# Tokens sorted into couples of passes that share a matrix, a first product by features, and a first tile that is turned before it is centred

## The chip, the cores and the metric

The kernel runs on one core of a Trainium2 chip. Its time is the device time of one execution in microseconds; the median of three runs before the change is 277.46 us (276.93 to 278.12). A core has five engines, each with its own queue that is worked in order: TensorE (PE; its weight loads are PEld), VectorE (DVE), ScalarE (ACT), GpSimd (POOL) and SyncE (SP), and 16 DMA engines that all queues share.

## The reference

There are 2,048 tokens of 512 features, and four matrices of 512x512, `ctx_2048[e]`. The first half is a gated product in which a token's id picks its matrix, used three times; the second half is a routed feed-forward layer. Cut to what is computed:

```python
x = x + tanh(g_xattn[0]) * xattn(layernorm(x), itok, ctx, ctx, ctx)
x = x + tanh(g_ffn[0]) * ffn(layernorm(x), w1, w3, w2, wr)

def xattn(h, token_ids, Wg, Wu, Wd):     # Wg = Wu = Wd = ctx, 4 experts
    e = minimum(clip(token_ids, 0, 24999) // 6250, 3)
    for each expert e:                   # tokens of other experts keep their own
        g = silu(h @ Wg[e].T); u = h @ Wu[e].T
        out[tokens of e] = (g * u) @ Wd[e].T

def ffn(x, w1, w3, w2, wr):
    p = softmax(x @ wr.T);  r, idx = top_k(p, 2);  gates = r / sum(r)
    h = silu(silu(x @ w1.T) @ w3.T) @ w2.T
    for k in range(2):
        out = out.at[idx[:, k]].add(gates[:, k:k+1] * h)   # idx is 0 to 7
```

Since g and u use one matrix, with z = h @ W.T the middle is silu(z) * z. The last loop adds into rows 0 to 7 of the output alone.

## The kernel before

**Sorting.** The core counts the tokens of each expert and gives each token a place, so that whole tiles of 128 places belong to one expert. There are 17 passes of 128 places: 13 with one expert (numbers below `NF` = 13) and 4 mixed ones, in which each quarter of 32 places has its own expert. The sums that give the places are a row of small VectorE steps (L205 to L253); `padded` is the place of each token. Then the compares `at_lane` (L258) and `what` (L267, L270) make one-hot tables, and 16 small matmuls into `tok` (L276) turn them round, so that `from_row` (L286) holds the token number of each lane of each pass. `which0` (L245) and `which` (L300) hold the matrix's first row for each place. `busy(n)` puts in n matmuls whose result nobody reads.

**A pass** p of the gated product has these steps, each a function:

- `gather(p)`: POOL fetches the pass's 128 token rows by an indirect DMA into x (pool `xp`, five buffers); `load(p)`: SP reads the matrix number and starts the load of one matrix of 1 MB, or four (pool `mp`, seven buffers).
- `centre(p)`: VectorE takes the moments of x and subtracts the mean: h. `scale` and `norms` work out the inverse root of the variance, rs, in a chain of nine small VectorE steps (`inverse_roots`, L355 to L373); in the loop two chains, for two tiles, are interleaved.
- `turn_in(p)`: TensorE turns h by four transposes (tp_a), ScalarE copies them to hT. The first tile has a form of its own, `first_in` (L415 to L428), in two halves.
- `up(p)`: z = h @ W.T by `expert_product` (L453): four matmuls with the turned tokens as the stationary operand and 512 columns of the matrix moving; the profile has two records for each. A mixed pass has sixteen, with 32 tokens each. Then ScalarE's Silu (L466), with rs as its scale, and VectorE's product with z and rs (L467): g.
- `turn_mid(p)`: TensorE turns g (tp_g), ScalarE copies it to gT (L473).
- `down(p)`: y = gT's product with the same matrix, VectorE adds it to x (L481), POOL stores the rows (L482).
- `norms(p_in, p_out)`: the moments of the new x, the two inverse roots (for this tile and for the one that comes in), and the normed tile h_f (L505). `turn_out(p)` turns it (tp_f), and ScalarE copies it to hT2, from which the feed-forward layer works.

**The order of the work** is written out by hand and is the order of each engine's queue. After the first two passes, a loop over i does, for the i-th pass of the list `order`: `up(i)`, `turn_in(i+1)`, `centre(i+2)`, `gather(i+3)`, `load(i+3)`, `down(i-1)`, `turn_out(i-2)`, `norms(i+2, i-1)`, `turn_mid(i)`. `step()` mixes in parts of the feed-forward layer as soon as half of the tokens are there (from i = 10): first layer by seven products of sums (`first_layer`, whose w1 sums are made in rounds 5 to 8), then `second_layer`, whose last part is the end of the kernel. w1 and wr are loaded in round 2, w3 and w2 in round 7. `tg` (tanh of the two gates) is a ScalarE step that waits for two tiny loads.

Of the kernel before, what the change touches and what calls it, by code (L numbers as in the profile page):

```python
# [19 lines left out]
P = 128  # L20
# [5 lines left out]
def tile_gated_moe_ffn(  # L26
# [39 lines left out]

    nc = tc.nc
# [7 lines left out]
    NF = NJ - (E - 1)  # L75
    G = P // Q
# [8 lines left out]
    mp = ctx.enter_context(tc.tile_pool(name="mp", bufs=7))  # L85
    xp = ctx.enter_context(tc.tile_pool(name="xp", bufs=5))
# [11 lines left out]
        "lane", "atlane12", "atlane4", "passes", "what", "place", "over", "rank_in", "incl",  # L98
        "keep", "cum", "hot", "before", "later", "stepped", "behind", "ones", "place0", "number",
        "idt", "pad", "psum", "padded", "lanes", "inpass",  # L100
# [26 lines left out]
    ones_f = ct_([P, 2 * E], F32, "ones_f")  # L127
    nc.vector.memset(ones_f, 1.0)
    extra = ct_([P, 2, E], F32, "extra")
    nc.vector.memset(extra[:, 0, :], 0.0)  # L130
    nc.vector.memset(extra[:, 1, :], float(Q - 1))
    whole = ct_([P, 2, E], I32, "whole")
    nc.vector.memset(whole[:, 0, :], -P)
    nc.vector.memset(whole[:, 1, :], -Q)
    cut = ct_([P, 2 * E + 1], F32, "cut")
# [5 lines left out]
    steps = ct_([P, 2 * E - 1], F32, "steps")  # L141
    nc.vector.memset(steps, float(D))
    nc.vector.memset(steps[:, E - 1 : E], float(-(E - 1) * D))
# [7 lines left out]
    H = 12  # L151
# [46 lines left out]
    def busy(n):  # L198
# [12 lines left out]
    num = ct_([P, 2, E], I32, "num")  # L211
    nc.vector.tensor_tensor(
        num, incl[:, :, NJ - 1].unsqueeze(1).to_broadcast([P, 2, E]), extra, ALU.add
    )

    size = ct_([P, 3, E], I32, "size")
    nc.vector.tensor_tensor(size[:, 0:3:2, :], num, whole, ALU.bitwise_and)
    nc.vector.tensor_sub(size[:, 1, :], size[:, 2, :], size[:, 0, :])

    def wide(a):  # L220
# [6 lines left out]
        cut[:, 1 : 2 * E + 1], ones_f, size[:, 0:2, :].rearrange("p h e -> p (h e)"),  # L227
        0.0, ALU.mult, ALU.add,
# [3 lines left out]
    over = ct_([P, E, NJ], F32, "over")  # L232
    nc.vector.tensor_tensor(over, rank_in, wide(size[:, 0, :]), ALU.is_ge)
    jump = ct_([P, E], F32, "jump")
    nc.vector.tensor_sub(jump, cut[:, E : 2 * E], cut[:, 1 : E + 1])
    place = ct_([P, E, NJ], F32, "place")
    nc.vector.tensor_tensor(place, rank_in, wide(cut[:, 0:E]), ALU.add)
    nc.vector.tensor_tensor(over, over, wide(jump), ALU.mult)

    start = ct_([P, 2 * E - 1], F32, "start")  # L240
    nc.vector.scalar_tensor_tensor(start, cut[:, 1 : 2 * E], 0.0, steps, ALU.is_le, ALU.mult)
    nc.vector.tensor_add(place, place, over)
    which0 = ct_([P, 1], I32, "which0")
    with nc.allow_low_precision("whole numbers below 4096"):
        nc.vector.tensor_reduce(which0, start, AX.X, ALU.add)  # L245
    nc.vector.tensor_mul(place, place, hot)
# [7 lines left out]
    atlane = [ct_([P, P, n], F16, f"atlane{n}") for n in (H, NJ - H)]  # L254

    def at_lane(h):
        j, n = (0, H) if h == 0 else (H, NJ - H)
        return nc.vector.tensor_tensor(  # L258
            atlane[h],
            lane[:, :, 0:n],  # L260
            lanes[:, j : j + n].unsqueeze(1).to_broadcast([P, P, n]),
            ALU.is_equal,
        )

    at_lane(0)
# [7 lines left out]
    at_lane(1)  # L273
    tok = ps_x.tile([P, NP], F32, tag="x", name="tok")
    for j in range(NJ):
        nc.tensor.matmul(  # L276
            tok, atlane[j // H][:, :, j % H], what[:, :, j], start=(j == 0), stop=(j == NJ - 1)
        )

    which = ct_([P, NU], I32, "which")  # L280
    later = ct_([P, 2 * E, NU], F32, "later")
    stepped = ct_([P, 2 * E - 1, NU], F32, "stepped")

    busy(21)
# [4 lines left out]
        place0.unsqueeze(1).to_broadcast([P, 2 * E, NU]),  # L289
        cut[:, 1 : 2 * E + 1].unsqueeze(2).to_broadcast([P, 2 * E, NU]),  # L290
# [4 lines left out]
        later[:, 0 : 2 * E - 1],  # L295
        steps.unsqueeze(2).to_broadcast([P, 2 * E - 1, NU]),
# [8 lines left out]
    def row_tables():  # L305
# [6 lines left out]
        nc.vector.tensor_sub(pads, size[:, 2, :], num[:, 0, :])  # L312
# [3 lines left out]
            later[:, E : 2 * E, NF:NU],  # L316
# [21 lines left out]
    def moments(xt, name):  # L338
        st = small.tile([P, 6], F32, tag="st", name=f"st_{name}")
        nc.vector.bn_stats(st, xt)  # L340
        mv = small.tile([P, 2], F32, tag="mv", name=f"mv_{name}")
        nc.vector.bn_aggr(mv, st)
        return mv

    def inverse_roots(mvs_, names):


        n = range(len(names))

        def new(tag):  # L350
            return [small.tile([P, 1], F32, tag=tag, name=f"{tag}_{name}") for name in names]

        v, r, q, w, rs = new("v"), new("r"), new("q"), new("w"), new("rs")
        for i in n:
            nc.vector.tensor_scalar_add(v[i], mvs_[i][:, 1:2], EPS)  # L355
        for i in n:
            nc.vector.tensor_scalar(
                r[i].bitcast(I32), v[i].bitcast(I32), -0.5, float(0x5F3759DF), ALU.mult, ALU.add
            )
        for i in n:  # L360
            nc.vector.scalar_tensor_tensor(q[i], r[i], v[i], r[i], ALU.mult, ALU.mult)
        for i in n:
            nc.vector.tensor_scalar(w[i], q[i], 0.375, -1.25, ALU.mult, ALU.add)
        for i in n:
            nc.vector.tensor_scalar(w[i], w[i], q[i], 1.875, ALU.mult, ALU.add)
        for i in n:
            nc.vector.tensor_mul(r[i], r[i], w[i])
        for i in n:
            nc.vector.scalar_tensor_tensor(q[i], r[i], v[i], r[i], ALU.mult, ALU.mult)
        for i in n:  # L370
            nc.vector.tensor_scalar(q[i], q[i], -0.5, 1.5, ALU.mult, ALU.add)
        for i in n:
            nc.vector.tensor_mul(rs[i], r[i], q[i])  # L373
        return rs
# [8 lines left out]
    order = [0, 1, 2, 3, 4, 5, NF, 6, 7, 8, NF + 1, 9, 10, NF + 2, 11, 12, NF + 3]  # L383
    assert sorted(order) == list(range(NP))
    xs, x1s, mvs, rss, hs, hTs, gTs, gs, hs2, mats = {}, {}, {}, {}, {}, {}, {}, {}, {}, {}

    def gather(p):
        xt = xp.tile([P, D], F32, tag="x", name=f"x_{p}")
        nc.gpsimd.indirect_dma_start(  # L389
            out=xt,  # L390
            out_offset=None,
            in_=x,
            in_offset=bass.IndirectOffsetOnAxis(ap=from_row[:, p : p + 1], axis=0),
        )
        xs[p] = xt

    def centre(p):

        mvs[p] = moments(xs[p], f"a{p}")
        hs[p] = work.tile([P, D], F32, tag="h", bufs=4, name=f"h_a{p}")  # L400
        nc.vector.tensor_scalar(hs[p], xs[p], mvs[p][:, 0:1], None, ALU.subtract)  # L401

    def scale(*ps):
        for p, rs in zip(ps, inverse_roots([mvs.pop(p) for p in ps], [f"a{p}" for p in ps])):
            rss[p] = rs
# [6 lines left out]
    def first_in(p):  # L412

        st = small.tile([P, 6], F32, tag="st", name=f"st_a{p}")
        nc.vector.bn_stats(st, xs[p])  # L415
        mvs[p] = small.tile([P, 2], F32, tag="mv", name=f"mv_a{p}")
        nc.vector.bn_aggr(mvs[p], st)
        hTs[p] = work.tile([P, KC * P], F32, tag="hT", bufs=2, name=f"hT_{p}")
        n = D // 2
        for i in range(2):  # L420
            h = work.tile([P, n], F32, tag="h", bufs=4, name=f"h_a{p}_{i}")
            nc.vector.tensor_scalar(
                h, xs[p][:, i * n : (i + 1) * n], mvs[p][:, 0:1], None, ALU.subtract
            )
            tp = ps_tp.tile([P, n], F32, tag="tp", name=f"tp_a{p}_{i}")
            for k in range(n // P):
                nc.tensor.transpose(tp[:, k * P : (k + 1) * P], h[:, k * P : (k + 1) * P], ident)
            nc.scalar.copy(hTs[p][:, i * n : (i + 1) * n], tp)  # L428

    def load(p):  # L430

        n0, n = (p, 1) if p < NF else (NF + (p - NF) * G, G)
        mats[p] = []
        for i in range(n0, n0 + n):
# [9 lines left out]
            mats[p].append(m)  # L444
# [16 lines left out]
    def up(p, inside=None):  # L461
        z = ps_mm.tile([P, D], F32, tag="mm", name=f"z_{p}")
        expert_product(z, hTs.pop(p), p, inside)
        g = work.tile([P, D], F32, tag="g", bufs=2, name=f"g_{p}")
        rs = rss.pop(p)
        nc.scalar.activation(g, z, AF.Silu, scale=rs)  # L466
        nc.vector.scalar_tensor_tensor(g, z, rs, g, ALU.mult, ALU.mult)  # L467
        gs[p] = g

    def turn_mid(p):  # L470
        tp = transposed(gs.pop(p), f"g{p}")
# [20 lines left out]
    def norms(p_in, p_out):  # L492


        if p_out is None:
            return
        xt = x1s.pop(p_out)
        mv = [moments(xt, f"f{p_out}")]
        names = [f"f{p_out}"]
        if p_in is not None:  # L500
            mv.append(mvs.pop(p_in))
            names.append(f"a{p_in}")
        rs = inverse_roots(mv, names)
        h = work.tile([P, D], F32, tag="h", bufs=4, name=f"h_f{p_out}")
        nc.vector.tensor_scalar(h, xt, mv[0][:, 0:1], rs[0], ALU.subtract, ALU.mult)  # L505
        hs2[p_out] = h
        if p_in is not None:
            rss[p_in] = rs[-1]
# [212 lines left out]
    def second_layer(b, g):  # L721
# [61 lines left out]
        a = work.tile([P, D], F32, tag="g", bufs=2, name="a")  # L783
# [52 lines left out]
    row_tables()  # L836
    positions.close()
# [125 lines left out]
```

## Time and profile before

| | before |
|---|---|
| time, median of three runs | 277.46 us (276.93 to 278.12) |
| profiled execution | 277.53 us |
| its span, first to last instruction | 275.8 us |
| granted TensorE clock | 1.00 |
| first gather issued, landed | 9.35, 12.87 us |
| first product z begins | 15.44 us |
| first product y begins | 24.02 us |
| output tile ready | 272.65 us |
| DMA | 42.54 MB, of it 29 matrices of 1 MB |

Times within the profile count from the start of the span. "Busy" is the time in which an engine works on an instruction. The chain of work is followed back from the last instruction: at each step to what released it, or to the instruction before it on its engine. In names, out<-in are the program's tiles; `128*128 128x512` is a stationary operand of 128 rows and columns and a moving one of 512 columns. An x after a name counts records.

### The profile page before, as it was taken

What the parts mean: (1) busy time and instruction counts of PE and PEld (TensorE: products, weight loads), DVE (VectorE), ACT (ScalarE), POOL (GpSimd) and SP (SyncE); (2) the same over time, 40 slices, a digit from 0 to 9 for tenths busy, and PEclk for the clock granted to TensorE, in tenths of its full rate; (3) what the DMA queues carried; (4) which work ended last, traced back from release to release, by engine and by line L of the source; (5) the groups of instructions that cost most, each with busy time, mean ns of one, the idle gap of its engine ahead of it and who ended that gap; (6) DMA issues with size and microseconds to landing.
All of it is one profiled execution on the core that took longest, in us unless ns stands there. A gap on an engine that the chain in (4) does not pass through costs nothing.

```text
span 275.8 us, 3562 instructions
## 1 busy us (share of the span) xinstructions
PE 266.6 (97%) x1173; PEld 125.4 (45%) x1173; DVE 148.7 (54%) x593; ACT 69.3 (25%) x134; POOL 39.3 (14%) x63
## 2 busy tenths in 40 slices
PE   5889999999999999999999999999999999999994
PEld 2445455544355454444344444534245444344362
DVE  6677877777888769918263481516253620711000
ACT  2022232232232231223143232312113233311120
POOL 6520122221122211211110010101010000000000
PEclk9999999999999999999999999999999999999999
DMA  0697998545669996697304084001000000000000
GB/s 1 217 354 277 408 402 334 173 155 206 228 225 402 389 409 258 173 398 264 112 26 166 2 312 180 38 0 40 0 12 2 0 0 1 0 0 2 0 0 2
DMA packets 20722, 42.54 MB, mean 154 GB/s; under 512 B 2143, under 2 KB 2207, under 8 KB 20704
## 3 DMA queue, kind: packets, MB, share of 16 engines
q1 hardware_dynamic: 17952, 33.66, 34.0%
q0 software_dynamic: 2720, 8.65, 8.3%
q8 instruction: 9, 0.15, 0.2%
q14 instruction: 9, 0.07, 0.1%
q10 hardware_dynamic: 32, 0.01, 0.0%
HBM read 38.10 MB, written 4.47 MB: 154 GB/s over the span
## 4 chain that ended last, share of the span: by engine, by line
PE 94%; DVE 2%; DMA 2%; issue 1%; ACT 0%; DVEq 0%
PE z L453 22%; PE y L453 21%; PE v L730 20%; PE X L622 10%; PE Y L622 5%; PE tp_f L380 3%; PE tp_a L380 3%; PE tp_g L380 3%; PE Z L622 2%; PE acc L742 1%; PE lg L699 1%; DMA x<-in_x_dram,from_row 1%; DMA idt<-in_ids_dram 1%; PE accT L758 1%; PE o L814 0%
## 5 line engine op out<-in xcount | busy, mean ns | idle before, releaser
L453 PE MATMUL z<-m,hT 128*32 128x512 f32 (+1 forms) x232 | 61.8, 595 | 0.2 <-ACT hT L428 0.2
L453 PE MATMUL y<-m,gT 128*32 128x512 f32 (+1 forms) x232 | 61.4, 594 | 0.0
L730 PE MATMUL v<-w,s 128*128 128x512 f32 (+1 forms) x136 | 57.3, 570 | 0.0
L730 PEld LDWEIGHTS v<-w,s 128*128 128x128 f32 x136 | 25.0, 190 | 27.2 <-issue 26.7
L453 PEld LDWEIGHTS z<-m,hT 128*32 128x32 f32 (+1 forms) x232 | 22.6, 146 | 29.5 <-issue 28.1
L453 PEld LDWEIGHTS y<-m,gT 128*32 128x32 f32 (+1 forms) x232 | 22.6, 146 | 27.8 <-issue 27.8
L482 POOL DMA_INDIRECT out_dram<-x,to_row x17 | 17.2, 1011 | 84.9 <-DVE x L481 82.7
L389 POOL DMA_INDIRECT x<-in_x_dram,from_row x17 | 16.7, 984 | 77.5 <-DVE h_a L401 22.9
L467 DVE SCALAR_TENSOR_TENSOR g<-z,rs_a,g 128x512 f32<-128x512 f32 x17 | 12.7, 750 | 27.1 <-ACT g L466 27.0
L466 ACT ACTIVATE g<-z,rs_a 128x512 f32<-128x512 f32 x17 | 11.7, 687 | 51.3 <-PE z L453 51.3
L481 DVE SCALAR_TENSOR_TENSOR x<-y,tg,x 128x512 f32<-128x512 f32 x17 | 12.7, 749 | 16.9 <-PE y L453 16.8
L738 ACT ACTIVATE s<-v 128x512 f32<-128x512 f32 (+1 forms) x17 | 9.7, 572 | 41.9 <-PE v L730 41.9
L515 ACT COPY hT<-tp_f 128x512 f32<-128x512 f32 x13 | 7.6, 587 | 43.5 <-PE tp_f L380 43.5
L340 DVE BATCH_NORM_STATS2 st_a<-x 128x6 f32<-128x512 f32 x16 | 11.0, 688 | 7.5 <-DMA x<-in_x_dram,from_row 7.5
L622 PE MATMUL X<-T,S 128*128 128x512 f32 x32 | 15.0, 592 | 0.0
L380 PEld LDWEIGHTS tp_f<-ident,h_f 128*128 128x128 f32 x68 | 8.2, 141 | 10.2 <-issue 10.2
L340 DVE BATCH_NORM_STATS2 st_f<-x 128x6 f32<-128x512 f32 x17 | 11.8, 695 | 0.6
L380 PEld LDWEIGHTS tp_a<-ident,h_a 128*128 128x128 f32 x64 | 7.7, 140 | 9.4 <-issue 9.1
L640 DVE TENSOR_TENSOR s<-X,c 128x512 f32<-128x512 f32 x4 | 2.8, 692 | 16.2 <-PE X L622 16.2
L473 ACT COPY gT<-tp_g 128x512 f32<-128x512 f32 x17 | 10.0, 586 | 5.3 <-PE tp_g L380 5.3
L380 PE MATMUL tp_f<-ident,h_f 128*128 128x128 f32 x68 | 10.4, 276 | 0.0
L380 PE MATMUL tp_g<-ident,g 128*128 128x128 f32 x68 | 10.2, 273 | 0.0
(165 smaller groups left out, 271.6 us busy)
## 6 DMA issues: line engine op xcount, KB each, us to landing
m<-in_ctxT_dram SPq DMA_DIRECT2D x29, 1024.0 KB
w<-in_w1T_dram SPq DMA_DIRECT2D x1, 1024.0 KB
w<-in_w3T_dram SPq DMA_DIRECT2D x1, 1024.0 KB
w<-in_w2T_dram SPq DMA_DIRECT2D x1, 1024.0 KB
x<-in_x_dram,from_row POOLq DMA_INDIRECT x17, 6.2
out_dram<-x,to_row POOLq DMA_INDIRECT x17, 6.1
wr<-in_wrT_dram SPq DMA_DIRECT2D x1, 64.0 KB
x_first<-out_dram SPq DMA_DIRECT2D x4, 4.0 KB
```

The source lines that it names most:

```text
L340: nc.vector.bn_stats(st, xt)
L380: nc.tensor.transpose(tp[:, k * P : (k + 1) * P], h[:, k * P : (k + 1) * P], ident)
L389: nc.gpsimd.indirect_dma_start(out=xt, out_offset=None, in_=x, in_offset=bass.IndirectOffsetOnAxis(ap=from_row[:, p : p + 1], axis=0),)
L453: nc.tensor.matmul(out_ps[i * n : (i + 1) * n, :], lhs[:, k * P + i * n : k * P + (i + 1) * n], m[:, k, :], start=(k == 0), stop=(k == KC ...
L466: nc.scalar.activation(g, z, AF.Silu, scale=rs)
L467: nc.vector.scalar_tensor_tensor(g, z, rs, g, ALU.mult, ALU.mult)
L473: nc.scalar.copy(gT, tp)
L481: nc.vector.scalar_tensor_tensor(xt, y, tg[:, 0:1], xt, ALU.mult, ALU.add)
L482: nc.gpsimd.indirect_dma_start(out=out, out_offset=bass.IndirectOffsetOnAxis(ap=to_row[:, p : p + 1], axis=0), in_=xt, in_offset=None, bou ...
L622: nc.tensor.matmul(out_ps, a[:, k, c * P : (c + 1) * P], bb[:, k, :], start=start and k == 0, stop=k == 1, skip_group_check=True,)
L730: nc.tensor.matmul(v, s1[:, k, c_b + t * P : c_b + (t + 1) * P], w3[:, k, c0 : c0 + n], start=(k == 0), stop=(k == KC - 1),)
L738: nc.scalar.activation(s2, v, AF.Silu)
```

## The change

**Couples.** `NC` = 10 of the one-expert passes now come in couples that have the same expert, so that one load serves both; 3 single passes and 4 mixed ones follow. The sizes have a third rank (multiples of 256, of 128, of 32), and the tables of places grow with it. `order` puts the first mixed pass fifth and a single pass last. Loads are listed in `units`, and `load_free` starts as many as there are free buffers.

**First product by features.** For one-expert passes except the first three of the order (`late`), `up` takes 128x128 blocks of the matrix as the stationary operand and the turned tokens, 128 columns, as the moving one: sixteen matmuls. z comes out turned, so `turn_mid` has nothing to do for it. As rs can't be applied to a turned tile by rows, these passes and the mixed ones are normed before the product, and their moments are taken one round earlier (`look_at`).

**Start.** The rows of the first pass get a table of their own (`tok0`, `from_row0`). The first tile is turned as it comes; its mean, spread to all partitions by a small matmul, is subtracted behind that. `inverse_roots` works on two columns at once.

```diff
-    order = [0, 1, 2, 3, 4, 5, NF, 6, 7, 8, NF + 1, 9, 10, NF + 2, 11, 12, NF + 3]
+    order = [0, 1, 2, 3, NF, 4, 5, 6, 7, NF + 1, 8, 9, NF + 2, 10, 11, NF + 3, 12]
+    NC = 2 * ((NT - E * (2 * P - 1) + 2 * P - 1) // (2 * P))
-    xp = ctx.enter_context(tc.tile_pool(name="xp", bufs=5))
+    xp = ctx.enter_context(tc.tile_pool(name="xp", bufs=6))
...
+    over = ct_([P, 2, E, NJ], F32, "over")
...
+    nc.vector.tensor_add(place, place, over[:, 1])
     nc.vector.tensor_mul(place, place, hot)
...
-    H = 12
+    H = 6
...
-    at_lane(0)
+    what0 = ct_([P, NJ], F16, "what0")
+    nc.vector.scalar_tensor_tensor(what0, inpass, 0.0, number, ALU.is_equal, ALU.mult)
+    at_lane = []
+    for i, j in enumerate(range(0, NJ, H)):
...
+    tok0 = ps_x.tile([P, 1], F32, tag="x", name="tok0")
+    for j in range(NJ):
+        nc.tensor.matmul(
+            tok0, at_lane[j], what0[:, j : j + 1], start=(j == 0), stop=(j == NJ - 1)
+        )
+    busy(3)
+    from_row0 = ct_([P, 1], I32, "from_row0")
+    nc.vector.tensor_scalar(from_row0, tok0, -1.0, 0.0, ALU.add, ALU.max)
...
-    busy(21)
+    busy(10)
...
+    def inverse_roots(var, name):
+        n = var.shape[1]
...
+        def square():
+            if n == 1:
+                nc.vector.scalar_tensor_tensor(q, r, v, r, ALU.mult, ALU.mult)
+            else:
+                nc.vector.tensor_mul(q, r, r)
+                nc.vector.tensor_mul(q, q, v)
...
+    def normed(p, xt, mv, rs, name):
+        h = work.tile([P, D], F32, tag="h", bufs=3, name=f"h_{name}{p}")
+        if rs is None:
+            nc.vector.tensor_scalar(h, xt, mv[:, 0:1], None, ALU.subtract)
+        else:
+            nc.vector.tensor_scalar(h, xt, mv[:, 0:1], rs, ALU.subtract, ALU.mult)
+        return h
...
     def first_in(p):
+        n = D // 2
+        raw = work.tile([P, KC * P], F32, tag="h", bufs=3, name=f"raw_{p}")
+        for i in range(2):
+            tp = ps_tp.tile([P, n], F32, tag="tp", name=f"tp_a{p}_{i}")
+            for k in range(n // P):
+                c = i * n + k * P
+                nc.tensor.transpose(tp[:, k * P : (k + 1) * P], xs[p][:, c : c + P], ident)
+            nc.scalar.copy(raw[:, i * n : (i + 1) * n], tp)
+        total = small.tile([P, 1], F32, tag="total", name="total")
+        nc.vector.tensor_reduce(total, xs[p], AX.X, ALU.add)
+        spread = ps_y.tile([P, P], F32, tag="y", name="spread")
+        nc.tensor.matmul(spread, total.to_broadcast([P, P]), ident, start=True, stop=True)
...
+        for i in range(2):
+            half = slice(i * n, (i + 1) * n)
+            nc.vector.scalar_tensor_tensor(
+                hTs[p][:, half].rearrange("p (k t) -> p k t", t=P),
+                spread.unsqueeze(1).to_broadcast([P, n // P, P]),
+                -1.0 / D,
...
+            )
...
+    units = []
+    for p in order:
+        if p >= NF:
+            units.extend(((p,), NF + (p - NF) * G + i) for i in range(G))
+        elif p >= NC:
+            units.append(((p,), p))
+        elif p % 2 == 0:
+            units.append(((p, p + 1), p))
...
+    def load_free(i):
+        n = len(loaded)
+        while n < len(units) and (
+            n < MP or max(order.index(p) for p in units[n - MP][0]) < i
+        ):
+            n += 1
+        load(n - len(loaded))
...
     def up(p, inside=None):
+        turned = p < NF and p not in late
+        if turned:
+            for c in range(KC):
+                for k in range(KC):
+                    nc.tensor.matmul(
+                        z[:, c * P : (c + 1) * P],
+                        mats[p][0][:, k, c * P : (c + 1) * P],
+                        hT[:, k * P : (k + 1) * P],
+                        start=(k == 0),
+                        stop=(k == KC - 1),
+                    )
+        else:
+            expert_product(z, hT, p, inside)
...
+        if p in late:
...
+        else:
+            nc.scalar.activation(g, z, AF.Silu)
+            nc.vector.tensor_mul(g, z, g)
+        (gTs if turned else gs)[p] = g
...
+    def look_at(p):
+        pairs[p] = pair_of(p)
+        mvs[p] = pairs[p][:, 1]
+        moments(xs[p], mvs[p], f"a{p}")
...
+    load(1)
+    for p in order[0:3]:
+        gather(p)
+    first_in(order[0])
...
+    moments(xs[order[0]], mvs[order[0]], "a0")
+    nc.vector.tensor_copy(rows_on, from_row)
+    nc.vector.tensor_copy(held[0:1, 1:NU], which[0:1, 1:NU])
+    for p in order[3:6]:
+        gather(p)
...
+    moments(xs[order[1]], mvs[order[1]], "a1")
+    centre(order[1])
+    scales(order[0], order[1])
+    moments(xs[order[2]], mvs[order[2]], "a2")
+    centre(order[2])
+    load(1)
...
+    up(order[0], inside=lambda: turn_in(order[1]))
     row_tables()
...
+    load_free(1)
     up(order[1], inside=lambda: turn_mid(order[0]))
     turn_in(order[2])
+    moments(xs[order[3]], mvs[order[3]], "a3")
+    scales(order[2], order[3])
     centre(order[3])
+    look_at(order[4])
...
         if i + 3 < NP:
-            gather(order[i + 3])
-            load(order[i + 3])
+            look_at(order[i + 3])
+        if i + 4 < NP:
+            gather(order[i + 4])
         if i <= NP:
             down(order[i - 1])
+        load_free(i)
...
-        if 5 <= i < 9:
+        if 6 <= i < 10:
             next(summing)
-        if i == 2:
+        if i == 4:
             w1 = load_w(w1T, "w1")
             wr = load_w(wrT, "wr")
-        if i == 7:
+        if i == 8:
             w3 = load_w(w3T, "w3")
+        if i == 12:
             w2 = load_w(w2T, "w2")
```

## The prediction

> **What bounds the kernel now.** First the page: its engine line and the slices. TensorE is busy 97% of the span at full clock; VectorE is busy seven or eight tenths in the first half, ScalarE and the DMA engines far less.
>
> ```profile
> PE 266.6 (97%) x1173; PEld 125.4 (45%) x1173; DVE 148.7 (54%) x593; ACT 69.3 (25%) x134; POOL 39.3 (14%) x63
> PE   5889999999999999999999999999999999999994
> DVE  6677877777888769918263481516253620711000
> PEclk9999999999999999999999999999999999999999
> ```
>
> Second, TensorE's waits: all of them. After 15.44 us only one of 0.3 us at the very end is left, so behind the start the time is the sum of what TensorE is given.
>
> ```profile
> PE tp_a L427 <- DVE h_a L422: 1.2, 1, 1.2
> PE o L814 <- DVE aT L800: 0.3, 1, 0.3
> PE z L453 <- ACT hT L428: 0.2, 1, 0.2
> ```
>
> Third, the chain of work in order of time (start, us): the start, and then one round of the loop.
>
> ```profile
> 9.35 3.52 DMA x<-in_x_dram,from_row
> ...
> 12.89 0.70 DVE st_a L415
> ...
> 15.44 2.84 PE z L453 x6
> 18.29 0.44 PE tp_a L380 x4
> ...
> 43.82 0.44 PE tp_g L380 x4
> 44.25 3.44 PE z L453 x8
> 47.69 0.44 PE tp_a L380 x4
> 48.13 3.44 PE y L453 x8
> 51.56 0.44 PE tp_f L380 x4
> 52.00 0.44 PE tp_g L380 x4
> ```
>
> A round is 3.44 + 3.44 for two products (four matmuls each, of two records) and three turns of 0.44: 8.19 us. The turn tp_g is what most passes lose.
>
> Fourth, the timeline of weight loads and matmuls where a matmul is too short to hide its load (accT, 8 columns).
>
> ```profile
> 270.71 0.52 PEld L758 LDWEIGHTS accT<-g,s 128*128 128x128 f32 x4 [0.23 <-ACT s L738]
> 270.71 0.61 PE L758 MATMUL accT<-g,s 128*128 128x8 f32 x4
> ```
>
> One load has 0.19 us, so the fourth starts at 0.52 - 0.19 = 0.33: three steps of 0.11. That is a load's own pace.
>
> **What the Trainium skill says.** "TensorE: Matmul & The Clock Gate", LDWEIGHTS: a load costs its columns at 1.2 GHz, 107 ns for 128; the trace's 110 agrees. Same page, The mechanism: loads overlap matmuls in flight only where the row group differs. Here the trace disagrees: four f32 turns (128 rows, a new load each) take 0.44, 0.109 each, where load plus stream would be near 0.2. "VectorE: DVE Perf Modes", errata section: a fixed extra time per instruction; the trace agrees (128x1 takes 0.15, 128x512 0.69). "DMA: Bandwidth & Descriptors", Anatomy of one DMA: 2.0 us + bytes / 436e3, an estimate of 2.6 for the 256 KB gather; the trace's 3.52 is used.
>
> **The change, part by part.**
>
> *Turned passes.* Of the 13 one-expert passes all but the first three, so 10, make their first product by features. Removed: tp_g, 10 x 0.44 = -4.4 us, and its ScalarE copy, which was hidden. Changed: 8 records of 512 columns become 32 of 128 with a load each. By streaming 3.44 / 32 = 0.1075, by the load's pace 0.11, by four turns 0.109. I take 0.1105: 3.54 a product, +0.10 x 10 = +1.0. Bounds: 0.1075 (nothing) and load and stream in turn, 0.215 (+34). Normalising before the product moves a multiplication from the g step to the h step; VectorE hides it.
>
> *VectorE's round.* g 0.70, h_a 0.54, moments 0.69 + 0.2, x 0.75, moments 0.9, roots, h_f 0.54. Roots become one chain of 11 two-wide steps of about 0.19 (steps of 0.15 plus the wait between, from 14.61 to 16.30), 2.15 against 1.95 for 18 interleaved. Sum 6.5 us, in the four rounds with a sum of w1 7.2, against a round of 3.54 + 3.44 + 2 x 0.44 = 7.86. A turned g is ready about 5.4 after the product two before it ended (x, moments, roots, h_f: 4.35; g), and y needs it at 12; h_f is needed 8 later. Hidden. Without that cover VectorE would set the round.
>
> *Couples.* 24 matrices are loaded instead of 29: -5 MB that nobody waits for (no TensorE wait on m). SP's queue: w1 (moved two rounds later) stands behind two loads that wait for products; it has two rounds before its first sum, and 1 MB needs some 3 us at the 400 GB/s of the page's slices. w3 and w2 move later too, to rounds 8 and 12, and are wanted from 160 us. Nothing. Five early gathers become six, x has a sixth buffer, and each later gather is issued a round ahead, as before. The last three early ones now wait for a copy of the table that stands behind the first moments on VectorE (15.6 instead of 13.4); behind them on POOL is only x0's store, wanted at 28, and pass 3's moments run at 24. Nothing.
>
> *The start.* VectorE: two `over` steps of 128 instead of 64 elements (+0.07 each) and one more dependent addition (+0.26): `padded` at 6.05 instead of 5.66. what0 +0.16, partly hidden: the first compare at 6.70 instead of 6.23. Compares of 768, 768 and 512: 0.47 + 0.47 (half of the 0.88 that 1536 took) + 0.42, done 8.06. tok0's last matmuls and the read 0.48, from_row0 0.17, issue 0.29: the gather at 9.0 instead of 9.35. The second gather waits for the whole table: compare and product 0.76, 16 matmuls 1.0, from_row: 10.85, as now (10.83). Landing 3.52 later, 12.5; the first matrix's load is 0.14 later and may still be in the way, so 12.6. VectorE is through with the longer tables (0.51, 0.49, 0.70, scaled by elements) at 12.25. TensorE's filler has 10 x 0.215 from 10.35 and ends then too.
>
> From landing to z0: now 2.57 (moments 0.9, h_a 0.6, turn, copy). New: the sum of 512 elements 0.68 (as BATCH_NORM_STATS2), the small product 0.6 (as from h_a's end at 14.43 to the copy's start at 15.02), the first half's subtraction 0.48, 0.05: 1.85; the turns and copies (0.5 + 0.75) run beside it. z0 starts at 14.45, -1.0.
>
> Behind z0's third step stands tp_a of pass 1, now at 18.29, new at 14.45 + 2.84 = 17.3. VectorE: second half 14.65, moments 0.85, two copies 0.2 (the matrix table now goes through VectorE, moved past POOL), moments 0.9, h_a: 17.03. Cover 0.3. Then roots 2.15 to 19.1, while z0 ends at 18.6: its Silu waits 0.5; moments and h_a of pass 2 fill until 20.5; g0 at 21.2, where tp_g0 is wanted at 21.2. No cover: what is late there shifts y0. The gates' loads are issued at 16.6 and 17.1 (now 16.68, 17.22) behind one matrix, wanted at 27. I take -0.9 of the start; bounds -1.1 and 0.
>
> **Sum:** -4.4 + 1.0 - 0.9 = -4.3 us. The profiled execution took 277.53 (span 275.8, 1.7 around it): 273.2. The median, 277.46, is 0.07 lower, less than these sums are good for.
>
> **The rivals.**
> 1. *The start gives nothing* (chance 0.12): tp_a1 and tp_g0 wait for VectorE, whose work before g0 grew by the roots' wider chain and a pass's moments. For: covers of 0.3 and 0. Against: row tables moved behind g0. -3.4: 274.1.
> 2. *VectorE sets the early rounds* (0.09): 7.2 of 7.86, without room for a late gather. For: seven to nine tenths busy there. If the eight rounds before the feed-forward work give back 0.25 each: 275.2.
> 3. *Loads half hidden* (0.08): 0.115 to 0.12 a record, +2.4 to +4.0 instead of +1.0: 274.6 to 276.2.
> 4. *Slower: loads not hidden* (0.05): in the features' product each 128-column record waits for its own load. The sum turns at 0.1075 + 5.3 / 320 = 0.124 a record. Fully in turn 0.215: 0.1075 x 320 = +34.4 - 5.3, 306.6. For: the skill's sentence, and the turns are another kind of matmul (0.14 us a load against 0.19). Against: with 256 columns the next load starts as the matmul does, and accT's loads follow at 0.11, not 0.19.
> 5. *More* (0.06): 0.1075 a record and -1.0 at the start: 272.1.
> That the change doesn't do what it says: the built program has ten products of 16 matmuls of 128 columns, seven tp_g, 24 matrix loads; this is excluded.
>
> **How the numbers follow.** The forecast, 273.2, has 0.58, waits unseen that cost over 6 us 0.02. The forecast's own range is 272.3 to 274.2. About 0.5% (1.4 us) is what a measurement can tell. Faster than 276.1: the forecast, 1, 5 and most of 2 and 3, 0.88; within: the rest of 2 and 3, 0.05; slower: 4 and the unseen, 0.07. The range 271.9 to 276.0 leaves out 4, some of 3 and the far ends.
>
> **What the changed profile would show.** z of turned passes in 3.5 us with 32 records, tp_g x28 records instead of 68; rounds of 7.9; the first gather at 9.0, z0 at 14.4, y0 at 23.1 instead of 24.0; no wait of TensorE in the loop. Wrong if z takes over 4 us, if TensorE waits for g or h in the loop, or if tp_g0 stays at 22.

## The result and the profile after

The changed kernel took 273.73 us (median of 4; 273.66 to 273.96), the kernel before beside it 277.56. The ratio is 0.9864, with a 95% interval of 0.9842 to 0.9887: 3.8 us, or 1.4%, faster. The forecast was 273.2. On another chip the ratio was 0.9843 (0.9823 to 0.9863). The profiled execution took 273.66 us, its span is 271.9.

First the page of the changed kernel: its engine line, and three rows of slices.

```profile
PE 264.2 (97%) x1383; PEld 142.2 (52%) x1383; DVE 146.5 (54%) x498; ACT 63.5 (23%) x124; POOL 39.1 (14%) x61
PE   5999999999999999999999999999999999999994
DVE  6697986864888989936263471417244521701000
PEclk9999999999999999999999999999999999999998
```

TensorE is as full as before, with more and shorter records (1383 instead of 1173). So the time is still what TensorE is given. Its waits, all but one that ends before the first table:

```profile
PE z L522 <- DVE hT L471: 0.6, 1, 0.6
PE tp_a L462 <- DMA x<-in_x_dram,from_row: 0.4, 1, 0.4
PE o L908 <- DVE aT L894: 0.3, 1, 0.3
```

None lies in the loop. The first turn now waits for the gather itself instead of for VectorE's centring, and the first product for the late subtraction. The chain in order of time (start, us), the start and one round:

```profile
8.76 3.54 DMA x<-in_x_dram,from_row
...
12.44 0.63 PE tp_a L462 x4
13.07 0.50 PE spread L467 x2
...
13.66 0.44 DVE hT L471
...
14.14 2.84 PE z L522 x6
16.99 0.55 PE tp_a L407 x4
...
21.09 0.63 PE tp_g L407 x4
...
23.01 3.44 PE y L522 x8
...
67.03 0.44 PE tp_f L407 x4
67.46 3.57 PE z L537 x32
71.04 0.44 PE tp_a L407 x4
71.47 3.44 PE y L522 x8
74.91 0.44 PE tp_f L407 x4
75.35 3.57 PE z L537 x32
```

y0, at 23.01, starts 1.01 us earlier than before. A round of a turned pass is 75.35 - 67.46 = 7.89 us instead of 8.19; between tp_f and z there is no tp_g. The timeline of one product by features, weight loads above, matmuls below:

```profile
34.79 3.65 PEld L537 LDWEIGHTS z<-hT,m 128*128 128x128 f32 x32
34.90 3.74 PE L537 MATMUL z<-hT,m 128*128 128x128 f32 x32
```

The last of 32 loads (0.19 us long) starts at 3.65 - 0.19 = 3.46: 31 steps of 0.1116 us. TensorE's time from one record's start to the next, summed by tile from y0 (the first pass's product y) to the step that makes the output tile, gives this account (us):

| | before | after | |
|---|---|---|---|
| tp_g | 7.27 | 2.62 | -4.65 |
| z, all one-expert passes | 37.89 | 39.36 | +1.47 |
| tp_f | 7.65 | 7.93 | +0.28 |
| all else | 195.63 | 195.82 | +0.19 |
| sum | 248.44 | 245.73 | -2.71 |

With 1.00 of the start (by the records' own starts) and 0.17 behind the output tile that is the span's 3.9.

### The profile page after: what moved, and what is told of

The parts are those of the page before. It is cut to its first block, busy times and chain, and to the rows that moved or that the text cites. A ratio compares the mean times of both kernels' runs of the same rounds, so it can differ in the third digit from the quotient of the medians.

```text
span 271.9 us, 3831 instructions
## 1 busy us (share of the span) xinstructions
PE 264.2 (97%) x1383; PEld 142.2 (52%) x1383; DVE 146.5 (54%) x498; ACT 63.5 (23%) x124; POOL 39.1 (14%) x61
## 3 DMA queue, kind: packets, MB, share of 16 engines
HBM read 32.86 MB, written 4.47 MB: 137 GB/s over the span
## 4 chain that ended last, share of the span: by engine, by line
PE 96%; DMA 2%; DVE 1%; issue 0%; DVEq 0%
PE y L522 22%; PE v L824 20%; PE z L537 13%; PE X L716 10%; PE z L522 9%; PE Y L716 5%; PE tp_f L407 3%; PE tp_a L407 3%; PE Z L716 3%; PE idle L212 2%; PE acc L836 1%; PE lg L793 1%; DMA x<-in_x_dram,from_row 1%; PE tp_g L407 1%; PE accT L852 1%; DMA idt<-in_ids_dram 1%
## 5 line engine op out<-in xcount | busy, mean ns | idle before, releaser
L537 PEld LDWEIGHTS z<-hT,m 128*128 128x128 f32 x320 | 36.8, 192 | 1.6 <-issue 1.4
L537 PE MATMUL z<-hT,m 128*128 128x128 f32 x320 | 37.5, 275 | 0.0
L522 PE MATMUL y<-m,g 128*128 128x512 f32 x80 | 36.1, 594 | 0.0
L522 PE MATMUL z<-m,hT 128*32 128x512 f32 (+1 forms) x152 | 25.7, 596 | 0.6 <-DVE hT L471 0.6
L522 PE MATMUL y<-m,gT 128*32 128x512 f32 (+1 forms) x152 | 25.4, 595 | 0.0
L418 POOL DMA_INDIRECT x<-in_x_dram,rows_on x14 | 14.4, 1027 | 63.0 <-DVE x L571 19.6
L522 PEld LDWEIGHTS y<-m,g 128*128 128x128 f32 x80 | 14.4, 190 | 15.2 <-issue 15.2
L555 DVE TENSOR_TENSOR g<-z,g 128x512 f32<-128x512 f32 x14 | 9.6, 688 | 22.0 <-ACT g L554 22.0
L522 PEld LDWEIGHTS z<-m,hT 128*32 128x32 f32 (+1 forms) x152 | 7.9, 122 | 13.8 <-issue 10.6
L522 PEld LDWEIGHTS y<-m,gT 128*32 128x32 f32 (+1 forms) x152 | 8.1, 122 | 12.1 <-issue 12.0
```

The costliest lines, as they stand in the source:

```text
L418: nc.gpsimd.indirect_dma_start(out=xt, out_offset=None, in_=x, in_offset=bass.IndirectOffsetOnAxis(ap=from_row0 if p == order[0] else (fro ...
L522: nc.tensor.matmul(out_ps[i * n : (i + 1) * n, :], lhs[:, k * P + i * n : k * P + (i + 1) * n], m[:, k, :], start=(k == 0), stop=(k == KC ...
L537: nc.tensor.matmul(z[:, c * P : (c + 1) * P], mats[p][0][:, k, c * P : (c + 1) * P], hT[:, k * P : (k + 1) * P], start=(k == 0), stop=(k = ...
L555: nc.vector.tensor_mul(g, z, g)
```

## The experiments

Chips differ a little, so each run has the kernel before beside it on the same chip, and ratios are to that one. It took 278.95 us beside four runs (tokens as the stationary operand, the first tile centred, one table, one load for each pass), 278.94 beside three others (more filler, the first couple, g0 earlier for the second time), and 277.65 beside the rest. The changed kernel itself was run with the three others: 274.45. Differences in us below are to this figure; the first four runs are on another chip, where the kernel before is equally fast.

**Tokens as the stationary operand again.**

```diff
-        turned = p < NF and p not in late
+        turned = False
```

> All passes make their first product with the turned tokens as the stationary operand, as before the change; couples, loads, norms ahead of the product and the start stay. My theory (the gain of the loop is ten turns of 0.44 us less ten products that are 0.13 us dearer): +3.0 us against the changed kernel, 276.7 us, and ten more tp_g of 0.44 us in the chain. Rival (the loop's gain comes from the rest: fewer loads, shorter VectorE chains): within 0.5 us of the changed kernel, 273.7 us.

277.41 us, ratio 0.9943 (0.9926 to 0.9960), where the changed kernel has 274.45 and 0.9843: +3.0. The loop from y0 to the output takes 249.05 us instead of 245.73 (0.3 of it is a stop at lg, the small matmuls of the routing; more at the end). In the chain of this run the turn tp_g is back between tp_f and z, in the round in which the changed kernel goes from tp_f at 67.03 straight to z at 67.46:

```profile
67.73 0.44 PE tp_f L407 x4
68.17 0.44 PE tp_g L407 x4
68.60 3.44 PE z L522 x8
```

The rival falls: with the couples, the fewer loads and the shorter VectorE work kept, the loop has nothing left of its gain (the kernel before has 248.44). It is the turns.

**What sets the pace of the new product.**

```diff
+            nc.tensor.matmul(z, ident, mats[p][0][:, 0, :], start=True, stop=True)
...
-                        z[:, c * P : (c + 1) * P],
+                        z[:, c * P : c * P + P // 2],
...
-                        hT[:, k * P : (k + 1) * P],
+                        hT[:, k * P : k * P + P // 2],
```

> The ten products by features take 64 columns of the turned tokens instead of 128, behind one matmul of 512 columns (0.86 us) that fills the tile; the first product of the other 64 tokens is left out. Theory A (a record of 128 columns costs a weight load's pace, 0.111 us, and streaming is hidden under it): z stays at 3.57 + 0.86 us, the whole at 273.7 + 8.6 = 282.3 us. Theory B (streaming sets the pace, 0.1075 us and a small fixed cost): z takes 1.8 + 0.86 us, the whole at about 264.6 us. Theory C (load and stream follow each other in part): in between.

281.81 us in a single execution, near theory A's 282.3. The timeline of the same place in this run, and the chain:

```profile
34.96 1.02 PE L535 MATMUL z<-m,ident 128*128 128x512 f32 x2
35.82 3.68 PE L538 MATMUL z<-hT,m 128*128 128x64 f32 x32
```

```profile
35.12 0.86 PE z L535 x2
35.98 3.52 PE z L538 x32
```

Half the columns, and 32 records take 3.68 us against 3.74, by the chain 3.52 against 3.57. From the second record on, the step from one to the next is 0.111 to 0.112 us, as with 128 columns. Theory B's 1.8 is out, and C's values between the two as well. The pace is that of the weight loads, and 128 columns stream beneath them.

**The first tile centred, then turned.** `first_in` has its form of before again, h in two halves that are then turned:

```diff
-    first_in(order[0])
     both = {p: pair_of(p) for p in order[0:4:2]}
...
     moments(xs[order[0]], mvs[order[0]], "a0")
+    first_in(order[0])
```

> The first tile is centred on VectorE and then turned, as before the change; its rows still come from the table of their own. My theory: from the landing to the first z 2.57 us instead of 1.84, of which 0.2 was lost again to the late g0: +0.5 to +0.7 us against the changed kernel, 274.3 us. Rival (the start is set by VectorE's roots and moments before g0, and turning earlier buys nothing): within 0.2 us, 273.8 us.

277.01 us, ratio 0.9927: +2.6 us against 274.45, far more than either theory. In the profiled executions 2.0 of it stand at y0; the other 0.6 are stops at lg and at o, which the edit doesn't touch. TensorE's longest wait before z0 (the first pass's product z), the chain, and the page's clock row:

```profile
PE tp_a L463 <- DVE h_a L458: 2.1, 1, 2.1
```

```profile
12.79 0.70 DVE st_a L372
...
13.74 0.36 DVE h_a L458
...
15.11 4.30 PE z L508 x6
19.41 0.44 PE tp_a L407 x4
...
25.10 3.44 PE y L508 x8
```

```profile
PEclk9979999999999999999999999999999999999999
```

From landing (12.77) to z0 it is 2.34 us instead of 1.8: half a microsecond more, where 0.7 were expected. But then the first three steps of z take 4.30 us instead of 2.84. TensorE had been idle for 2.1 us, from 12.17 to 14.24, and the clock's record in the trace stands at 0.5 from 14.66 to 18.07 us. That was a cause I had not named, so I tried it by itself.

**The same, with more filler ahead of it.**

```diff
-    busy(10)
+    busy(18)
     from_row = ct_([P, NP], I32, "from_row")
```

> The first tile centred and then turned, with 18 instead of 10 matmuls of filler ahead of it, so that TensorE idles under 1 us instead of 2.1 before the first turn. My theory (1.5 us of that run's loss was TensorE's half clock for 3.4 us after the idle time): the clock stays full, the first three steps of z take 2.84 us instead of 4.30, y0 at 23.4 to 23.6 instead of 24.9, +0.5 to +0.7 us against the changed kernel. Rival (the loss is VectorE's and the gather's): z's steps at 2.84 us, but y0 stays above 24.3.

```profile
12.57 0.70 DVE st_a L372
...
13.51 0.36 DVE h_a L458
...
14.89 2.84 PE z L508 x6
17.73 0.44 PE tp_a L407 x4
...
23.42 3.44 PE y L508 x8
```

The clock stays whole (its row on the page has 9 throughout), z's steps have 2.84 us again, and in the chain y0 is at 23.42, instead of 25.10 without the filler and 23.10 in the changed kernel beside it. So of the 2.0 us by which y0 was late, 1.7 are gone. 1.46 of these are z's steps, that is the clock; the other 0.2 are that VectorE began with the rows at 12.57 instead of 12.79, which the filler does not explain. Turning the tile as it comes is worth the 0.3 us that is left at y0. The whole time, 275.47 us (0.9870), is 1.0 above the changed kernel's: the rest lies in stops at lg and at the tail (4.86 us for lg against 4.47, 1.62 for o against 1.32), which the edit doesn't touch. The changed kernel, with its filler of 10 matmuls, can do without the other 8 because TensorE waits only 0.4 us for its first turn.

**One table for all passes.**

```diff
-    what0 = ct_([P, NJ], F16, "what0")
...
-    tok0 = ps_x.tile([P, 1], F32, tag="x", name="tok0")
...
-                ap=from_row0
-                if p == order[0]
-                else (from_row if p in order[1:3] else rows_on)[:, p : p + 1],
+                ap=(from_row if p in order[0:3] else rows_on)[:, p : p + 1],
```

> No table of its own for the first pass: tok0, what0 and from_row0 are gone, all rows come from one table, which is then ready earlier than in the changed kernel. My theory: the first gather is issued at 9.2 to 9.3 us instead of 8.76, and all behind it moves: +0.4 to +0.5 us, 274.2 us. Rival (the gather then finds the first matrix's load out of its way, or the second gather's earlier issue pays): 0, 273.7 us.

275.11 us (0.9863; 0.9831 to 0.9895), 0.7 above 274.45, so the theory's direction and somewhat more. Chain:

```profile
9.55 3.46 DMA x<-in_x_dram,from_row
...
14.85 2.84 PE z L514 x6
```

The gather comes 0.79 later than 8.76, where 0.4 to 0.5 were expected, and z0 0.71 later. The interval is too wide for the time alone to decide; the trace does. It also has a stop of 1.1 us at lg, 0.4 more than the changed kernel's own run beside 278.94.

**One load for each pass.**

```diff
-        elif p >= NC:
-            units.append(((p,), p))
-        elif p % 2 == 0:
-            units.append(((p, p + 1), p))
+        else:
+            units.append(((p,), p))
```

> Couples are kept in the sorting, but each pass loads its own matrix: 29 loads instead of 24. My theory (nobody waits for a matrix): 0, within 0.4 us of 273.7, no wait of TensorE on m. Rival (the couples' saved loads are part of the gain, since gathers share the DMA engines with them): +0.5 us or more, with VectorE or TensorE waiting for x or m.

281.61 us, ratio 1.0089 (1.0066 to 1.0112): slower than the kernel before, though its 17 executions scatter more than any other's, from 278.91 to 282.94. My theory falls. The longest wait of TensorE, the chain, and the clock row of this run:

```profile
PE z L520 <- DMA m<-in_ctxT_dram: 3.7, 1, 3.7
```

```profile
15.99 6.07 DMA m<-in_ctxT_dram
...
22.20 4.51 PE z L520 x6
...
28.44 3.44 PE y L520 x8
...
65.41 9.81 DMA x<-in_x_dram,rows_on
```

```profile
PEclk9997999999999999999999999999999999999999
```

Pass 1 has to have a matrix of its own, and the change has put its look-up behind VectorE's first moments, so that it is issued at 15.99 us and lands at 22.06 (before: issued at 11.16). TensorE waits 3.7 us, and here too its clock is at a half for 3.4 us afterwards, from 22.44 on: y0 is 5.4 us late. Later a gather takes 9.8 us; the longest in the changed kernel takes 8.7.

**Only the first couple shares.**

```diff
-        elif p >= NC:
+        elif p > 1:
             units.append(((p,), p))
-        elif p % 2 == 0:
-            units.append(((p, p + 1), p))
+        elif p == 0:
+            units.append(((0, 1), 0))
```

> As the run with one load for each pass, but passes 0 and 1 share theirs: 28 loads. My theory now (the couple's worth is at the start alone: it lets the second matrix's look-up stand behind VectorE's first moments): y0 at 23 us instead of 28.3, no wait of TensorE on m; what the 4 other loads cost in the loop stays as in that run, 1.6 us, so +1.6 us against the changed kernel. Rival (all of the single loads' cost comes from DMA traffic): y0 late by several us again.

275.57 us (0.9879), +1.1 against the changed kernel. There is no wait for m, and in the chain y0 is in its old place:

```profile
22.74 0.44 PE tp_a L407 x4
23.18 3.43 PE y L522 x8
```

So the first couple is worth 5 to 6 us, nearly all at the start. The other four loads cost 1.1, where I had expected 1.6; tp_f is 0.9 us longer in sum than in the changed kernel (8.81 against 7.92). Of this, 0.53 is one stop behind a tp_f, at 75.58 us, for which the trace names no releaser; that it comes from late gathers through VectorE is likely, but not shown. The rival, that traffic explains it all, is out.

**Two edits of order.** A mixed pass last, and g0 ahead of the third tile's centring:

```diff
-    order = [0, 1, 2, 3, NF, 4, 5, 6, 7, NF + 1, 8, 9, NF + 2, 10, 11, NF + 3, 12]
+    order = [0, 1, 2, 3, NF, 4, 5, 6, 7, NF + 1, 8, 9, NF + 2, 10, 11, 12, NF + 3]
```

```diff
-    centre(order[2])
     load(1)
...
     up(order[0], inside=lambda: turn_in(order[1]))
+    centre(order[2])
     row_tables()
```

> The last two passes of the order change places, so that a mixed pass is last, as before the change. My theory (each change of TensorE from 32-column to 128-column stationary operands costs 0.15 us, and a mixed pass that is last saves two of them): -0.3 us, 273.4 us. Rival (the chain's 0.15 is put elsewhere then): 0.

> VectorE centres the third tile after the product g0 instead of before it. My theory: tp_g0 has waited about 0.2 us for g0; now g0 is ready at 20.5 instead of 20.9 us: -0.2 us, 273.5 us. Rival (tp_a of the third tile then waits instead): 0 or more.

> The two edits of order together. My theory: -0.5 us, 273.2 us, faster than both kernels. Rival: within 0.2 us of the changed kernel.

> The edit that puts g0 ahead of the third tile's centring, again, now beside the changed kernel on one chip: -0.2 us (273.5 where the changed kernel has 273.7), from z0 to y0 8.5 instead of 8.7 us. Rival: no difference beyond 0.1 us.

A mixed pass last: 273.75 us (0.9868), nothing. The sums by tile show acc, tp_a, y and the turned z together 0.3 us shorter, the expected amount, and o, at the tail, 0.3 longer behind a wait for a Silu. The run with both edits has that wait too, but so have the two runs with the first tile centred, where the order is the changed kernel's; whether it belongs to the order stays open. g0 earlier: 273.61 (0.9863), and beside the changed kernel on another chip 274.70 against 274.45. The chain of the first of these two:

```profile
14.31 2.84 PE z L522 x6
...
21.22 0.44 PE tp_g L407 x4
...
22.95 3.44 PE y L522 x8
```

In both traces y0 follows z0 after 8.64 us instead of the changed kernel's 8.87 (by the records' own starts 8.48 instead of 8.71), the expected 0.2, but the time doesn't show it. Both edits: 273.50 (0.9857; 0.9837 to 0.9878). The intervals overlap with the changed kernel's (0.9842 to 0.9887): no version here is shown to be faster than it.

## Why the prediction was right

**What bounds it** held: no wait in TensorE's loop, before or after. The sum of its work was the way to the number. (The list of waits there, called all of them, leaves out two that end before 8 us: 3.1 us for VectorE's hot and 0.9 for its table what. Nothing rests on them.)

**Turned passes.** The removed turns gave 4.65 us, forecast 4.4: tp_g to the next product takes 0.116 a record, not 0.109. The new product cost +0.147 a pass, forecast +0.10. The term that was mis-sized is the pace: the forecast took 0.1105, next to the load's own pace as read from three steps, 0.11; over 31 steps that pace is 0.1116, and the half-columns run shows that it is the load's. A z that follows tp_f directly adds 0.028 a pass, which the sum had left out. Together the loop gave 2.7 us instead of 3.4. That is more than the forecast's error of 0.5 us, and in part luck hid it: 0.17 us behind the output tile, which no part of the forecast speaks of, and about 0.1 at the start (below) went the other way. The rivals with loads not hidden, or half hidden, are out: the Trainium skill's sentence ("TensorE: Matmul & The Clock Gate", The mechanism) that loads overlap matmuls in flight only where the row group differs does not, taken alone, describe these f32 loads, which start 2 to 3 ns behind the start of the matmul ahead of them, with all 128 rows.

**VectorE's round** was covered as worked out, and the rival that has VectorE set the early rounds is out: TensorE's rounds of 7.89 us follow each other with nothing between, with VectorE six to nine tenths busy there. The first roots took 2.26 us (16.68 to 18.94), forecast 2.15.

**The start.** Forecast and measured: gather 9.0 and 8.76 (0.14 of the difference is that the ids came earlier), sum of the first tile 0.68 and 0.69, small product 0.6 and 0.65, subtraction 0.48 and 0.44, landing to z0 1.85 and 1.84, y0 23.1 and 23.01. The earlier ids are no work of the change: in the changed kernel's second profile y0 is at 23.10, in the first couple's at 23.18, so about 0.1 of the 1.0 us is chance. The 0.0 us of cover at tp_g0 was right to name: in the chain that turn takes 0.63 instead of 0.44, and with g0 ahead of the centring 0.2 us come back. What the step did not see is TensorE's clock. The new start leaves out 8 fillers of 31, and it works because TensorE waits for the gather for 0.4 us only; with the old first tile on the same filler the clock took 1.5 us. I had compared the filler's end with the landing for time alone.

**Couples** were costed at nothing. For the kernel before, its waits support that (none on m), though no run tried it. As a part of this change it was wrong. The step listed what was queued behind each load on SP, and the start's step noted that the matrix table now goes through VectorE, behind the first moments; what neither saw is that the second look-up hangs on that table, and that only a shared first matrix gives it the time. Without the couples the change would have been slower than before, a mechanism for "slower" that stood among none of the rivals.

## What to carry to other kernels

When the engine that bounds is full, sum its own instructions by tile and price each new one by its slower half: with 128x128 f32 blocks as stationary operand, the load sets the pace, and a moving operand of 128 columns fits beneath it. Ask of every part of a change what the other parts lean on: here the couples carried the late look-up, and the early turn carried the clock. An idle stretch of TensorE near its start can cost more than its length: here 2.1 us brought 1.5 more.

## What the runs showed of the hardware

- After 2.1 us without matmuls TensorE's granted clock fell to a half for 3.41 us, and three matmuls of 512 columns took 4.30 us instead of 2.84; after 1.2 us (the kernel before), 1.3 (one table) and 0.4 it stayed whole. The record of the clock changes on a grid of 3.41 us that starts with its first entry: 7.83 + 2 x 3.41 = 14.66 us in that run, 8.79 + 4 x 3.41 = 22.44 in the one with single loads. In the first run the whole idle time, 12.17 to 14.24, lies in the stretch of the grid that ends there; in the second 3.2 us of it do (18.52 to 22.20). Whether 2.1 us that fall into two stretches would do no harm was not tried. The Trainium skill ("TensorE: Matmul & The Clock Gate", What's actually happening) has windows of 3413 ns, which the 3.41 agrees with; it lets the clock fall after an idle window of about that length, and here 2.1 us were enough.
- A 128x128 f32 weight load has a pace of 0.1116 us. With a new load for each, matmuls of 64 columns are hardly faster than of 128: 3.52 against 3.57 us for 32.
- In six of the fourteen profiles TensorE stops at lg for 0.3 to 1.2 us in sum, always in the first of its two bursts, with no releaser in the trace. Its cause stays open; it is as large as the small edits of order that were tried, or larger, and hides them.
